# Outer token sums made by adding DMAs on seeded blocks instead of by GpSimd

## The chip, the cores and the metric

The kernel runs on one core of one Trainium2 chip. Its engines work side by side, each through its own list of instructions: PE (TensorE, matrix products), DVE (VectorE), ACT (ScalarE), POOL (GpSimd) and SP (SyncE, which here starts DMAs). All data transfers run on the core's 16 DMA engines. Engines wait for one another through semaphores, and the order on each engine is fixed when the kernel is built. The metric is the device time of the core in microseconds (us). A profiled execution gives the span from the first to the last instruction, and its own time is a little above the span.

## The reference

A layer norm over tokens, a gated linear recurrence, and a routed feed-forward block whose result is scattered by adding. Cut to what matters here:

```python
def _L0_attn_ref(u, a, b, c, d, gate_w, gate_b, d_lr_u, d_lr_v):
    g = jax.nn.sigmoid(jnp.einsum('btd,ed->bte', u, gate_w) + gate_b)
    u_g = u * g
    ...
def _L0_ffn_ref(x, w1, w3, w2, wr):
    xr = x.reshape(-1, D)
    route_probs = jax.nn.softmax(xr @ wr.T, axis=-1)
    routes_k, indices_k = jax.lax.top_k(route_probs, TOP_K)
    gates = routes_k / jnp.sum(routes_k, axis=-1, keepdims=True)
    h = jax.nn.silu(xr @ w1.T)
    h = jax.nn.silu(h @ w3.T)
    h = h @ w2.T
    out = jnp.zeros_like(xr)
    for k in range(TOP_K):
        out = out.at[indices_k[:, k]].add(gates[:, k:k + 1] * h)
    return out.reshape(B, S, D)
x = L0_attn_u                      # (4, 1024, 1024) float32
xn = _layernorm(x, axis=-1)
s = _L0_attn_ref(xn, ...)
g = _silu(_L0_ffn_ref(xn, ...))
x = x + s * g
```

The scatter uses the expert's number as the row, so with 8 experts only the first 8 rows of the 4096 receive anything; all the other rows of the result are rows of the input. The two large products, with `w1` and `w3`, are needed for every token all the same, since every token is added to one of those rows.

## The kernel before

**Work and tiles.** The 4096 tokens are taken in four groups, `sb` = 0 to 3, of 1024. For each group there are a `u` phase (tokens times `w1`, then silu) and an `m` phase (that result times `w3`, silu, then a small scatter product on PE, `acc`). Group 0 also carries the gate product, `g`, between its `u` halves. All values are float32. A *block* is a tile of 128 x 4 x 512 numbers (1 MB); there are 20 of them, `b`. A *quarter* is 128 x 512 (256 KB); there are 24, `q`. A block `o` has four quarters `o[:, 0]` to `o[:, 3]`.

**Fast multiplication in two levels.** Each phase multiplies a 2 x 2 matrix of token blocks (a11, a12, a21, a22; in the code `left[kind, sb, (I, J)]`) by a 2 x 2 matrix of weight blocks with seven products in place of eight. Such a product is a *half* (class `Half`), numbered 1 to 7, and it runs in seven steps, which are the same scheme once more on the quarters of its block; in groups 1 to 3 one of the seven inner products is cut a third time (`eighth`, with `token_thirds` and a weight part `w..._t` that is loaded by `load_thirds`). The halves go in the order 1, 2, 5, 6, 7, 4, 3 in a `u` phase and 1, 5, 6, 2, 7, 4, 3 in an `m` phase.

**Outer token sums.** Four of the halves need a sum of token blocks: half 5 needs s1 = a21 + a22, half 6 needs s2 = s1 - a11, half 3 needs s4 = a12 - s2, and half 7 needs s3 = a11 - a21. The functions `s1`, `s2`, `s4`, `s3` make them, four operations of 128 x 512 each, one for each quarter. In groups 1 to 3 they run on POOL (`s_engine`); s4 is made in place in the block of s2. In group 0 DVE makes them, partly through spare PSUM banks (`with_bank`).

**Inner token sums.** `left_sums` makes four sums of quarters for each half, on POOL in every group, and `token_thirds` three more operations on quarter 1 of the half's block. They read the outer sum, so for halves 3, 5, 6 and 7 they come after it. In the code's terms, `left_sums` is due six places before the half's start and `token_thirds` two before it. In groups 1 to 3 the weight sums come from DRAM: `load_kept` (1 MB, ten places ahead) and `load_kept_sum` (256 KB each).

**What sets the order.** One planner orders everything. `at(place, f, ...)` puts a function on a heap; a function that yields a number goes on so many places later; PE's steps call `run_todo`, and so all instructions of all engines get their order in the program. A half is seven places, and in groups 1 to 3 a place is 1.7 us of PE. A sum is visible to those that read it (`left[kind, sb, "s1"]`, and so on) when the function that makes it has come to its end in this plan; `left_sums` looks again every quarter of a place until it is. Places order the instructions; on the chip an engine runs its list as fast as its semaphores let it. An instruction that waits holds up all that stands behind it on its engine.

**Queues.** Every DMA before the last few is started by SP: loads of tokens for the next group, weights and weight sums, copies of rows of x into the result (`copy_rows`). SP keeps eight in flight; in the full stretches, each start waits for an earlier landing.

Of the kernel before, what the change touches and what calls it, by code (L numbers as in the profile page):

```python
# [13 lines left out]
AF = mybir.ActivationFunctionType  # L14
ALU = mybir.AluOpType
# [7 lines left out]
def kernel(  # L23
# [55 lines left out]
    class Pinned:  # L79
# [16 lines left out]
    pe, dve, act, pool, sync = (  # L96
        Pinned(e) for e in (nc.tensor, nc.vector, nc.scalar, nc.gpsimd, nc.sync)
    )
# [36 lines left out]
    def block(uses=1):  # L135
        return Held(blocks, uses)
# [50 lines left out]
    def at(place, f, *args):  # L187

        seq[0] += 1
        heapq.heappush(todo, (place, seq[0], f, args))  # L190
# [392 lines left out]
    def spare_bank(of=(0, 1)):  # L583


        while not any(n in free_banks for n in of):
            yield 0.25
        taken[0] = next(n for n in free_banks if n in of)
        free_banks.remove(taken[0])
# [3 lines left out]
    def bank_tile(n):  # L593
        if n == 2:
            return ps_sm.tile([P, H], F32, tag="sm", name="spare2")
        return acc if n == 0 else ps_acc.tile([P, H], F32, tag="rows", name="spare")

    def with_bank(out, p, q, order=(0, 1, 2, 3), swap=False, op=ALU.subtract, of=(0, 1)):


        for j in order:
            yield from spare_bank(of)
            n = taken[0]
            ps = bank_tile(n)
            act.copy(ps, q[:, j])
            yield 0.5
            a, b = (ps, p[:, j]) if swap else (p[:, j], ps)
            dve.tensor_tensor(out[:, j], a, b, op)
            free_banks.append(n)
            if of != (0, 1):  # L610
                yield 0.5
# [163 lines left out]
    left = {}  # L775
    left_q = {}

    def s_engine(kind, sb):
        return pool if sb > 0 else dve


    BANKS = {("u", 0): (0, 1), ("m", 0): (0,)}

    def s1(kind, sb, n):
        eng = s_engine(kind, sb)
        a21, a22 = left[kind, sb, (1, 0)], left[kind, sb, (1, 1)]
        o = block(1 + n)
        if (kind, sb) in BANKS:
            yield from with_bank(o, a21, a22, (3, 0, 1, 2), op=ALU.add, of=BANKS[kind, sb])
        else:  # L790
            for q in (3, 0, 1, 2):
                eng.tensor_tensor(o[:, q], a21[:, q], a22[:, q], ALU.add)
                if q == 0:
                    yield 0.5
        a21.drop()
        a22.drop()
        left[kind, sb, "s1"] = o

    def s2(kind, sb, n):
        eng = s_engine(kind, sb)  # L800
        while (kind, sb, "s1") not in left:
            yield 0.25
        p, a11 = left[kind, sb, "s1"], left[kind, sb, (0, 0)]
        o = block(2 * n)
        if (kind, sb) in BANKS:
            yield from with_bank(o, p, a11, (2, 3, 0, 1), of=BANKS[kind, sb])
        else:
            for q in (2, 3, 0, 1):
                eng.tensor_tensor(o[:, q], p[:, q], a11[:, q], ALU.subtract)
                if q == 3:  # L810
                    yield 0.5
        p.drop()
        a11.drop()
        left[kind, sb, "s2"] = o

    def s4(kind, sb, n):

        eng = s_engine(kind, sb)
        while (kind, sb, "s2") not in left:
            yield 0.25  # L820
        o, a12 = left[kind, sb, "s2"], left[kind, sb, (0, 1)]
        if (kind, sb) == ("m", 0):
            yield from with_bank(o, o, a12, (2, 3, 0, 1), True, of=(0, 2))
        else:
            for q in (2, 3, 0, 1):
                eng.tensor_tensor(o[:, q], a12[:, q], o[:, q], ALU.subtract)
                yield 0.5
        a12.drop()
        left[kind, sb, "s4"] = o

    def s3(kind, sb, n):
        eng = s_engine(kind, sb)
        a11, a21 = left[kind, sb, (0, 0)], left[kind, sb, (1, 0)]
        o = block(n)
        if (kind, sb) == ("m", 0):
            yield from with_bank(o, a11, a21, (2, 3, 0, 1), of=(0, 2))
        else:
            for q in (2, 3, 0, 1):
                eng.tensor_tensor(o[:, q], a11[:, q], a21[:, q], ALU.subtract)
                yield 0.5  # L840
        a11.drop()
        a21.drop()
        left[kind, sb, "s3"] = o
# [481 lines left out]
    for kind, sb, i, plain in line:  # L1325
# [3 lines left out]
        n = 2 if sb == 0 and kind == "u" and i not in PLAIN_G else 1  # L1329
# [12 lines left out]
    for sb in range(NS):  # L1342
        n = 2 if sb == 0 else 1
        U = {i: start["u", sb, i] for i in range(1, 8)}
        at(U[5] - (12 if sb > 1 else 7 if sb else 9), s1, "u", sb, n)
        at(U[5] - (9 if sb > 1 else 6), s2, "u", sb, n)
        at(U[7] - 10, s3, "u", sb, n)
        at(U[3] - (13 if sb == 0 else 8.6), s4, "u", sb, n)
        if sb == 0:
            at(U[5] + 2, route, sb)  # L1350
        M = {i: start["m", sb, i] for i in range(1, 8)}
        at(M[5] - 8, s1, "m", sb, 1)
        at(M[5] - 4, s2, "m", sb, 1)
        at(M[7] - 12, s3, "m", sb, 1)
        at(M[3] - 16, s4, "m", sb, 1)
        if sb > 0:
            for r in range(6 if sb < NS - 1 else 4):
                at(U[1] + 14 * r, copy_rows, 6 * (sb - 1) + r)
        if sb + 1 < NS:
            bcs = {}  # L1360
            at(M[1] - (46 if sb == 0 else 40), stats, sb + 1, bcs)
            for k, (I, J) in enumerate(HB):
                at(M[1] + (12 if sb == 0 else 4) + 3 * k, load_xn, sb + 1, I, J, USES[I, J])
            at(M[1] + (17 if sb == 0 else 4), norm, sb + 1, bcs)
            for IJ in HB:
                at(
                    M[1] + 26,
                    lambda sb=sb, IJ=IJ: left.__setitem__(
                        ("u", sb + 1, IJ), xn[(sb + 1,) + IJ]
                    ),  # L1370
                )
# [228 lines left out]
```

## Time and profile before

| | |
|---|---|
| median of 3 runs | 816.02 us (815.76 to 816.16) |
| profiled execution, its time | 816.45 us |
| its span | 814.6 us |
| granted TensorE clock, mean | 0.999 |
| from group 1's scatter to group 2's (286.25 to 460.92) | 174.67 us |
| the same, one group on (460.92 to 637.30) | 176.38 us |
| from there to 802.00 | 164.70 us |
| DMA, whole span | 203.95 MB, mean 250 GB/s |
| POOL, largest four groups, busy | 244.0, 184.5, 152.6, 72.7 us |
| ACT, largest group, mean of one | 696 ns, x152 |

Instructions are grouped by line, engine, operation and tile; since every instruction is recorded in one helper, all have line 89, and the groups are told apart by tile names and shapes: `b` is a block, `q` a quarter, `X`, `Y` and `Z` are the PSUM banks of the products, with the phase behind them (`X_m`). In a row, "out<-in", then the shapes, the count, the busy time and the mean duration in ns, then the engine's idle time ahead of these instructions and what ended it. A row of the timeline begins with the start and the duration in us. In the 40 slices of the page each digit is the busy share of a slice in tenths. A row of DMA issues ends with the median time from issue to landing.

### The profile page before, as it was taken

How to read it: one execution, taken by the hardware profiler on the slowest of the kernel's cores; microseconds unless marked ns; L12 is line 12 of the kernel's file. 1: busy time of each engine (PE TensorE's matmuls, PEld its weight loads, DVE VectorE, ACT ScalarE, POOL GpSimd, SP SyncE). 2: the span in 40 equal slices, each digit the busy share in tenths (PEclk: the TensorE clock that was granted, in tenths of full speed). 3: DMA queues.
4: the chain of work that ended last, by engine and by line, in shares of the span. 5: the costliest groups of instructions: out<-in, count | busy, mean ns of one | idle time of the engine just before them, and what ended most of it. 6: DMA issues, size and time to landing. Idle time of an engine off the chain costs nothing.

```text
span 814.6 us, 12336 instructions
## 1 busy us (share of the span) xinstructions
PE 804.0 (99%) x4337; PEld 698.3 (86%) x4337; DVE 513.9 (63%) x988; ACT 263.6 (32%) x458; POOL 642.2 (79%) x628
## 2 busy tenths in 40 slices
PE   8999999999999999999999999999999999999997
PEld 6888888888888878888888788888888788888884
DVE  5986598766488635744897246735894357656553
ACT  1245126876332228341022165421122021220111
POOL 2799796956999699799999962999498853997820
PEclk9999999999999999999999999999999999999999
DMA  9946609464988939659968967649957567766800
GB/s 336 421 180 233 232 28 359 183 245 138 401 298 284 350 123 341 257 177 389 364 222 325 372 236 263 226 177 388 368 196 291 173 221 244 229 199 203 337 1 2
DMA packets 61980, 203.95 MB, mean 250 GB/s; under 512 B 7152, under 2 KB 10464, under 8 KB 50272
## 3 DMA queue, kind: packets, MB, share of 16 engines
q1 hardware_dynamic: 61600, 202.63, 68.3%
q8 instruction: 35, 0.57, 0.3%
q10 hardware_dynamic: 320, 0.54, 0.2%
q14 instruction: 25, 0.20, 0.1%
HBM read 176.35 MB, written 43.54 MB: 270 GB/s over the span
## 4 chain that ended last, share of the span: by engine, by line
PE 89%; POOL 6%; issue 3%; DMA 2%; DVE 1%; ACT 0%; POOLq 0%; ACTq 0%
PE X_m L89 22%; PE X_u L89 20%; PE Z_m L89 11%; PE Z_u L89 11%; PE X_g L89 6%; PE Y_m L89 5%; PE Y_u L89 5%; POOL q L89 3%; PE Z_g L89 3%; POOL b L89 2%; PE acc L89 2%; PE plT L89 2%; DMA b<-in_x 2%; PE Y_g L89 1%; PE pp L89 0%
## 5 line engine op out<-in xcount | busy, mean ns | idle before, releaser
L89 POOL TENSOR_TENSOR q<-b 128x512 f32<-128x512 f32 (+2 forms) x224 | 244.0, 1106 | 53.3 <-DVE b L89 22.9
L89 ACT ACTIVATE b<-b 128x512 f32<-128x512 f32 (+1 forms) x152 | 105.3, 696 | 299.6 <-DVE b L89 289.3
L89 POOL TENSOR_TENSOR b<-b,b 128x512 f32<-128x512 f32 x120 | 152.6, 1294 | 61.5 <-PE X_u L89 30.0
L89 POOL TENSOR_TENSOR q<-b,q 128x128 f32<-128x128 f32 (+1 forms) x210 | 184.5, 892 | 8.0 <-issue 3.4
L89 PE MATMUL X_m<-q,q 128*128 128x256 f32 x448 | 106.0, 379 | 0.0
L89 PE MATMUL X_u<-q,q 128*128 128x256 f32 x432 | 102.4, 380 | 0.0
L89 PEld LDWEIGHTS X_m<-q,q 128*128 128x128 f32 x448 | 83.4, 190 | 11.3 <-issue 0.8
L89 DVE TENSOR_TENSOR b<-X_u,b 128x512 f32<-128x512 f32 x87 | 60.0, 689 | 51.4 <-PE X_u L89 49.8
L89 PEld LDWEIGHTS X_u<-q,q 128*128 128x128 f32 x432 | 80.2, 190 | 11.1 <-issue 1.2
L89 DVE TENSOR_TENSOR b<-X_m,b 128x512 f32<-128x512 f32 x88 | 60.4, 687 | 40.4 <-PE X_m L89 40.0
L89 POOL TENSOR_TENSOR q<-q,b 128x512 f32<-128x512 f32 x56 | 72.7, 1298 | 12.7 <-PE Z_u L89 12.1
L89 DVE TENSOR_TENSOR b<-b,bc 128x1024 f32<-128x1024 f32 x56 | 67.8, 1211 | 5.2 <-ACT bc L89 5.1
L89 DVE TENSOR_TENSOR b<-b,b 128x512 f32<-128x512 f32 x72 | 69.1, 963 | 3.0
L89 PE MATMUL X_u<-b,b 128*128 128x256 f32 x248 | 58.6, 380 | 0.2
L89 DVE TENSOR_TENSOR b<-Y_m,b 128x128 f32<-128x128 f32 (+1 forms) x112 | 41.4, 385 | 25.2 <-PE Y_m L89 14.8
L89 DVE TENSOR_TENSOR b<-Z_m,b 128x512 f32<-128x512 f32 x48 | 33.0, 688 | 38.1 <-PE Z_m L89 37.7
L89 DVE TENSOR_TENSOR b<-Z_u,b 128x512 f32<-128x512 f32 x47 | 32.4, 689 | 36.7 <-PE Z_u L89 35.8
L89 DVE TENSOR_TENSOR b<-Y_u,b 128x128 f32<-128x128 f32 (+1 forms) x111 | 40.9, 384 | 21.8 <-PE Y_u L89 13.2
L89 PE MATMUL Z_m<-b,q 128*128 128x256 f32 x224 | 53.1, 380 | 0.0
L89 PE MATMUL X_m<-b,b 128*128 128x256 f32 x224 | 53.0, 379 | 0.0
L89 PE MATMUL X_m<-q,b 128*128 128x256 f32 x224 | 53.0, 379 | 0.0
L89 PE MATMUL Z_m<-q,q 128*128 128x256 f32 x224 | 52.9, 379 | 0.0
(194 smaller groups left out, 1317.0 us busy)
## 6 DMA issues: line engine op xcount, KB each, us to landing
q<-w SPq DMA_DIRECT2D x168, 256.0 KB, 4.2
b<-in_w SPq DMA_DIRECT2D x36, 1024.0 KB, 14.9
b<-w_T SPq DMA_DIRECT2D x24, 1024.0 KB, 6.8
b<-in_xT SPq DMA_DIRECT2D x15, 1024.0 KB, 7.3
w<-q SPq DMA_DIRECT2D x56, 256.0 KB, 6.4
b<-in_x SPq DMA_DIRECT2D x12, 1024.0 KB, 10.2
w_T<-b SPq DMA_DIRECT2D x8, 1024.0 KB
q<-w_t SPq DMA_DIRECT2D x28, 256.0 KB, 3.9
```

The source lines that it names most:

```text
L89: r = f(*args, **kwargs)
```

## The change

In groups 1 to 3 the sums s1, s2, s3 and s4 are no longer made by POOL operations. ScalarE copies one of the two inputs into the sum's block, quarter by quarter, with a factor of 1 or -1, and one DMA of 1 MB, started from POOL's queue, adds the other input to what stands there (`accum_op=ALU.add`). That is 23 sums: the `u` phase's s1 of group 1 stays on POOL, with its quarters in another order. s4 takes a block of its own. In group 0 the sums are made as before. Most of the sums start earlier in the plan: in the `u` phases s1 by 5 places (groups 2 and 3), s2 by 4 (6 in group 1), s3 by 4 and s4 by 5.4; in the `m` phases s1 by 3, s2 by 2 and s3 by 3.

```diff
@@ -775,68 +775,87 @@
     left = {}
     left_q = {}
 
-    def s_engine(kind, sb):
-        return pool if sb > 0 else dve
-
 
     BANKS = {("u", 0): (0, 1), ("m", 0): (0,)}
 
+    def seeded(o, seed, sign, other, wait):
+
+        for q in range(4):
+            act.activation(o[:, q], seed[:, q], AF.Copy, scale=sign)
+            yield 0.5
+        while other not in left:
+            yield 0.25
+        yield wait
+        pool.dma_start(o.tile, left[other].tile, accum_op=ALU.add)
+
     def s1(kind, sb, n):
-        eng = s_engine(kind, sb)
-        a21, a22 = left[kind, sb, (1, 0)], left[kind, sb, (1, 1)]
+        a22 = left[kind, sb, (1, 1)]
         o = block(1 + n)
         if (kind, sb) in BANKS:
+            a21 = left[kind, sb, (1, 0)]
             yield from with_bank(o, a21, a22, (3, 0, 1, 2), op=ALU.add, of=BANKS[kind, sb])
+        elif (kind, sb) == ("u", 1):
+            a21 = left[kind, sb, (1, 0)]
+            for q in (3, 2, 0, 1):
+                pool.tensor_tensor(o[:, q], a21[:, q], a22[:, q], ALU.add)
+                yield 0.25
         else:
-            for q in (3, 0, 1, 2):
-                eng.tensor_tensor(o[:, q], a21[:, q], a22[:, q], ALU.add)
-                if q == 0:
-                    yield 0.5
+            yield from seeded(o, a22, 1.0, (kind, sb, (1, 0)), 1)
+            a21 = left[kind, sb, (1, 0)]
         a21.drop()
         a22.drop()
         left[kind, sb, "s1"] = o
 
     def s2(kind, sb, n):
-        eng = s_engine(kind, sb)
-        while (kind, sb, "s1") not in left:
-            yield 0.25
-        p, a11 = left[kind, sb, "s1"], left[kind, sb, (0, 0)]
-        o = block(2 * n)
-        if (kind, sb) in BANKS:
+        if sb > 0:
+            a11 = left[kind, sb, (0, 0)]
+            o = block(2 * n)
+            for q in range(4):
+                act.activation(o[:, q], a11[:, q], AF.Copy, scale=-1.0)
+                yield 0.5
+            while (kind, sb, "s1") not in left:
+                yield 0.25
+            yield 3 if (kind, sb) == ("u", 1) else 4
+            p = left[kind, sb, "s1"]
+            pool.dma_start(o.tile, p.tile, accum_op=ALU.add)
+        else:
+            while (kind, sb, "s1") not in left:
+                yield 0.25
+            p, a11 = left[kind, sb, "s1"], left[kind, sb, (0, 0)]
+            o = block(2 * n)
             yield from with_bank(o, p, a11, (2, 3, 0, 1), of=BANKS[kind, sb])
-        else:
-            for q in (2, 3, 0, 1):
-                eng.tensor_tensor(o[:, q], p[:, q], a11[:, q], ALU.subtract)
-                if q == 3:
-                    yield 0.5
         p.drop()
         a11.drop()
         left[kind, sb, "s2"] = o
 
     def s4(kind, sb, n):
 
-        eng = s_engine(kind, sb)
         while (kind, sb, "s2") not in left:
             yield 0.25
         o, a12 = left[kind, sb, "s2"], left[kind, sb, (0, 1)]
         if (kind, sb) == ("m", 0):
             yield from with_bank(o, o, a12, (2, 3, 0, 1), True, of=(0, 2))
+        elif sb > 0:
+            p, o = o, block()
+            yield from seeded(o, p, -1.0, (kind, sb, (0, 1)), 1)
+            p.drop()
         else:
             for q in (2, 3, 0, 1):
-                eng.tensor_tensor(o[:, q], a12[:, q], o[:, q], ALU.subtract)
+                dve.tensor_tensor(o[:, q], a12[:, q], o[:, q], ALU.subtract)
                 yield 0.5
         a12.drop()
         left[kind, sb, "s4"] = o
 
     def s3(kind, sb, n):
-        eng = s_engine(kind, sb)
         a11, a21 = left[kind, sb, (0, 0)], left[kind, sb, (1, 0)]
         o = block(n)
         if (kind, sb) == ("m", 0):
             yield from with_bank(o, a11, a21, (2, 3, 0, 1), of=(0, 2))
+        elif sb > 0:
+            yield from seeded(o, a21, -1.0, (kind, sb, (0, 0)), 1)
         else:
             for q in (2, 3, 0, 1):
-                eng.tensor_tensor(o[:, q], a11[:, q], a21[:, q], ALU.subtract)
+                dve.tensor_tensor(o[:, q], a11[:, q], a21[:, q], ALU.subtract)
                 yield 0.5
         a11.drop()
         a21.drop()
@@ -1342,16 +1361,16 @@
     for sb in range(NS):
         n = 2 if sb == 0 else 1
         U = {i: start["u", sb, i] for i in range(1, 8)}
-        at(U[5] - (12 if sb > 1 else 7 if sb else 9), s1, "u", sb, n)
-        at(U[5] - (9 if sb > 1 else 6), s2, "u", sb, n)
-        at(U[7] - 10, s3, "u", sb, n)
-        at(U[3] - (13 if sb == 0 else 8.6), s4, "u", sb, n)
+        at(U[5] - (17 if sb > 1 else 7 if sb else 9), s1, "u", sb, n)
+        at(U[5] - (13 if sb > 1 else 12 if sb else 6), s2, "u", sb, n)
+        at(U[7] - (14 if sb else 10), s3, "u", sb, n)
+        at(U[3] - (13 if sb == 0 else 14), s4, "u", sb, n)
         if sb == 0:
             at(U[5] + 2, route, sb)
         M = {i: start["m", sb, i] for i in range(1, 8)}
-        at(M[5] - 8, s1, "m", sb, 1)
-        at(M[5] - 4, s2, "m", sb, 1)
-        at(M[7] - 12, s3, "m", sb, 1)
+        at(M[5] - (11 if sb else 8), s1, "m", sb, 1)
+        at(M[5] - (6 if sb else 4), s2, "m", sb, 1)
+        at(M[7] - (15 if sb else 12), s3, "m", sb, 1)
         at(M[3] - 16, s4, "m", sb, 1)
         if sb > 0:
             for r in range(6 if sb < NS - 1 else 4):
```

## The prediction

> **What bounds the kernel now.** I read first the busy times, then the 40 slices, the groups and the DMA issues, then PE's idle time and the windows around it, and last the chain that leads into the sums concerned. The page, cut to those lines:
>
> ```profile
> PE 804.0 (99%) x4337; PEld 698.3 (86%) x4337; DVE 513.9 (63%) x988; ACT 263.6 (32%) x458; POOL 642.2 (79%) x628
> ...
> DMA  9946609464988939659968967649957567766800
> ...
> L89 POOL TENSOR_TENSOR b<-b,b 128x512 f32<-128x512 f32 x120 | 152.6, 1294 | 61.5 <-PE X_u L89 30.0
> ...
> b<-in_w SPq DMA_DIRECT2D x36, 1024.0 KB, 14.9
> b<-w_T SPq DMA_DIRECT2D x24, 1024.0 KB, 6.8
> b<-in_xT SPq DMA_DIRECT2D x15, 1024.0 KB, 7.3
> ```
>
> PE is busy 804.0 of 814.6 us at full granted clock. POOL, whose work is taken away, is a follower: its 79% cost nothing unless PE waits for it. Between 18 and 800 us the timeline of PE has one idle row:
>
> ```profile
> 561.57 0.46 PE L89 MATMUL Y_m<-q,q 128*128 128x128 f32 x2 [1.37 <-POOL b L89]
> ```
>
> The row names POOL, but POOL's token third for this matmul was done at 550.8. The other operand is a weight third, `w3_6_t`, whose load was issued at 550.2 and landed at 561.4 (11.2 us for 256 KB; the group's median is 4.2 or less in quiet stretches). So the one stall is a late DMA, and less POOL work cannot end it. The windows say why it is late (columns: stretch; length, then busy time and count of PE, PEld, DVE, ACT, POOL; granted clock, DMA share, GB/s):
>
> ```profile
> 360.00:370.00 10.00, 10.00 (x52) 8.79 (x51) 3.00 (x8) 3.34 (x7) 9.85 (x10) 1.00 0.66 224
> 370.00:380.00 10.00, 10.00 (x55) 8.99 (x54) 4.28 (x8) 2.69 (x5) 9.84 (x13) 1.00 0.96 370
> 530.00:540.00 10.00, 10.00 (x54) 8.89 (x53) 4.38 (x10) 3.11 (x5) 9.84 (x11) 1.00 0.01 2
> 540.00:550.00 10.00, 10.00 (x55) 8.99 (x54) 3.15 (x7) 2.38 (x4) 9.92 (x10) 1.00 1.04 386
> 550.00:560.00 10.00, 10.00 (x54) 8.94 (x52) 4.61 (x7) 2.25 (x4) 9.92 (x11) 1.00 0.85 342
> 560.00:570.00 10.00, 8.63 (x43) 7.54 (x43) 5.64 (x10) 1.18 (x2) 9.45 (x11) 1.00 1.04 409
> 720.00:730.00 10.00, 10.00 (x53) 8.99 (x54) 6.02 (x14) 1.91 (x4) 9.84 (x12) 1.00 0.50 172
> ```
>
> From 540 us the 16 DMA engines are full, after ten empty microseconds in which SP waits for the statistics. The same holds around 370 to 402 us one group earlier; group 3 has room (0.50). POOL is full in these stretches too. At the rate of a full stretch, some 409 GB/s, 1 MB takes 2.6 us of all 16 engines.
>
> **The change part by part.** *POOL loses* 23 sums of 4 operations: 92 x 1.294 = 119 us. PE's only gap is not POOL's, so this is worth 0 on the end. It is cover for what follows.
>
> *ScalarE gains* 92 copies of 128x512. The nearest row is an activation of that shape, 0.63 us (below), so 58 us on an engine that is busy 263.6 us and whose largest group waits 289 us for VectorE. The program order of the changed kernel, laid against the old one, is the same for PE, VectorE and SP; ScalarE has only these copies put in. They read blocks ready long before, so they wait for nothing, and a later activation is delayed by at most one or two, 0.63 to 1.3 us, under the 4 us of idle before the activations that matter. I take 0; without cover it would be 1.3 us twice per group.
>
> *DMA gains* 23 transfers of 1 MB that add to their target. None is in this trace. Time on the 16 engines: at least one pass, 2.6 us; with a second read of the target 5.2; with each pass by itself (two reads, one write) 7.8. I take 2.6 to 5.2. Time from issue to landing, D: below, the fastest plain 1 MB load (4.9 us, issued 540.0); above, the slowest in a full stretch (13.1 us, issued 550.8) plus a second pass, 15.7. In a quiet stretch I take 5.0 + 2.6 = 7.6, in a full one 10 to 13, as most rows of such stretches are (7.5 to 13.1 for loads behind others). The Trainium skill (DMA: Bandwidth & Descriptors, section "Issuing engines are not separate DMA queues") speaks against the change here: a DMA started from POOL runs on the same 16 engines as SP's and interleaves with them. The full windows above are where that would bite; no transfer of POOL is in this trace to show it. The same skill (Collectives: The Full Stack, section on the bandwidth ceiling) has an add read two sources on one ring, with a measured ratio of 1.93 to a plain copy; by it the quiet D would be an estimated 1.93 x 5.0 = 9.7 us and all terms below would lie in their upper halves; no row here has an add.
>
> *The new waits.* In the old kernel POOL adds a quarter as soon as its input is there. Now the whole sum starts with its last quarter and ends with a landing. That matters where the input is late: the `m` half 5, whose first sum needs the block (1,0) just out of ScalarE's silu:
>
> ```profile
> 357.77 0.63 ACT L89 ACTIVATE b<-b 128x512 f32<-128x512 f32 x1 [4.17 <-DVE b L89]
> ...
> 532.44 0.63 ACT L89 ACTIVATE b<-b 128x512 f32<-128x512 f32 x1 [4.17 <-DVE b L89]
> ...
> 708.82 0.63 ACT L89 ACTIVATE b<-b 128x512 f32<-128x512 f32 x1 [3.89 <-DVE b L89]
> ```
>
> These end at 358.4, 533.1 and 709.5; only then can the DMA of s1 go. What is queued behind it on POOL: the inner sums of half 5, which read the landed block, so POOL stands for D. Then come 11 operations (8.6 us by their old durations) in group 1, 7 (6.8 us) in groups 2 and 3, then the DMA of s2, another D, and behind that, since the next operation reads s2, two operations (2.5 us) that make half 5's third inner sum. PE wants that sum at 385.6, at 560.5 (561.9 less the stall) and at 736.8, and s2 itself at 383.4, 558.1 and 734.6. Group 1: 385.6 - 358.4 - 8.6 - 2.5 = 16.1 us are left for two landings, less 0 to 1.5 for issuing (two issues at up to 0.7, about twice an SP issue). Groups 2 and 3: 18.1 and 18.0, so 16.5 to 18.1. Hence the stall is 2D less these, and the point from which it bites is a mean D of 7.3 to 8.1 us in group 1, 8.2 to 9.1 in the others.
>
> - Group 1: s1 goes into a stretch of share 0.66, 7.6 to 10; s2 into one of 0.96, 10 to 13. Sum 17.6 to 23 less 14.5 to 16.1: 1.5 to 8.5 us. I take 3, the low side, as loads issued just ahead of it landed in 5.
> - Group 2: s1 meets the empty stretch, 7.6; s2, issued at about 548, the full one, 10 to 13. Sum 17.6 to 20.6 less 16.5 to 18.1: -0.5 to 4.1. In the same place the load that already stalls PE by 1.4 is behind s2's transfer and comes 2.6 to 5.2 later. Both delay the same matmuls, so the larger counts: 2.6 to 5.2; I take 4.
> - Group 3: 15.2 to 18 less 16.5 to 18: 0 to 1.5. I take 0.5.
>
> The other sums (all of the `u` phases, s3, s4) are first used 12 to 30 us after they could be issued, beyond the 10 to 13 of a full stretch: 0; with 15.7 still 0 to 4 in the tightest one. s4 takes a block of its own where it worked in place: SP's loads get waits on ScalarE's copies and on landings, all past by the old times but one load at 461.3 that waits to 464.0 and has 29 us to spare: 0. The moved starts change POOL's order only; no DMA of SP moves, so no queue is passed by another.
>
> Sum: 3 + 4 + 0.5 = 7.5 us. On the profiled execution 816.45 would be 824.0 (its span 814.6, with 1.85 around it); the median of the runs is 816.02, 0.43 less, so 823.5; an engine that is 99% busy makes nothing of it up, but the three terms can share half a microsecond with the 1.37 us already lost at 560, and I give 823.
>
> **The rivals.** *The cover holds, no change.* If the add runs along with the copy, D is near the plain 5 to 7 us, below the 7.3 from which anything is late, and only the load at 561 moves. Then 814.6 (the 1.37 us gone because the order of traffic changes) to 817.6 (one more pass before it); 816.0. For it: 5.0 us for the load of 364.8. Against: the full stretches, where 1 MB loads that were not first in line took 7.5 to 13. This is the case on the other side: not slower, one mechanism, with its point at D = 7.3.
>
> *Faster beyond what can be told.* 0.2% (1.6 us) is about what a measurement of this kernel can tell from no change. The single stall is 1.37 us, so this needs it gone and something in the first 18 or last 13 us besides, which the change doesn't touch. 814.
>
> *DMA becomes the bound.* DMA shares over the three periods are 0.77 of 174.7 us, 0.74 of 176.4 and 0.56 of 164.7: 134.5, 130.5 and 92.2 us. With 7, 8 and 8 sums at 5.2 us they become 171, 172 and 134: just under the periods. At 7.8 us they are 189, 193 and 155, and groups 1 and 2 are 14.5 and 16.5 too long: 816 + 31 = 847. For it: three passes are what the data needs if nothing overlaps. Between, with D = 13 in groups 1 and 2 and 10 in 3: 26.2 - 15.3, 26.2 - 17.3 and 20 - 17.3, or 10.9 + 8.9 + 2.7 = 22.5, 838.5.
>
> *It doesn't do what it says*: POOL may stand waiting for as long as it saves. POOL has 119 us less work and up to 23 x 10 of landings to wait for; but beyond the `m` half 5 the plan puts other work between, so this is in the terms already.
>
> **How the numbers follow.** Forecast (817.6 to 830, point 823): 0.48. Hidden: 0.27. DMA-bound or long D (830 to 850): 0.19. Faster: 0.06. So slower 0.67, same 0.27, faster 0.06. The range is 814.5 to 842: it takes in the hidden case and the middle of the long one, and leaves out the far end of that and of the faster one. The forecast's own range is 817.6 to 830.
>
> **What would show it.** In the changed profile: PE idle at about 385 and 560, ended by POOL or a DMA in `m` half 5 to 6; POOL idle for D after the silus at 358 and some 174 us later; adds landing in 7 to 8 us quiet and 10 to 13 in full stretches; DMA share up by 0.1 to 0.2 in each period; ScalarE up by about 58 us, POOL down by 119. I am wrong if adds land in under 7 us in the full stretches, if a load of weights sets the stalls instead, or if PE waits in a `u` phase.

## The result and the profile after

The changed kernel takes 840.6 us (839.12 to 842.87) beside 816.07 us before (the table's 816.02 with one more run): a ratio of 1.0304, 95% interval 1.0276 to 1.0331. It is 24.5 us slower, where 7 us was forecast. The profiled execution took 842.87 us, the slowest of four, with a span of 841.1 us, 26.5 us more than before. From its page:

```profile
PE 813.1 (97%) x4337; PEld 704.0 (84%) x4337; DVE 511.7 (61%) x988; ACT 310.0 (37%) x550; POOL 543.0 (65%) x559
...
DMA  9936629465987899799988999699989698875920
...
q0 software_dynamic: 3312, 24.12, 14.1%
...
b<-in_w SPq DMA_DIRECT2D x36, 1024.0 KB, 18.2
...
b<-b POOLq DMA_DIRECT2D x23, 1024.0 KB, 11.3
```

POOL lost 99 us of work where 119 was forecast, because starting the 23 DMAs is work of its own, 0.85 to 1.01 us each. ScalarE gained 46 us where 58 was forecast. The new queue's packets filled 14.1% of 16 engines' span: 0.141 x 841.1 / 23 = 5.2 us of all 16 engines for each 1 MB add. In the windows over the three periods (286.18 to 468.36, 468.36 to 653.88, 653.88 to 824.67 us) the DMA share is 0.90, 0.95 and 0.73, where it was 0.77, 0.74 and 0.56.

PE, which had one idle row between 18 and 800 us, now has eight. Its timeline, each row that begins behind idle time:

```profile
386.37 0.89 PE L89 MATMUL X_m<-b,b 128*128 128x256 f32 x3 [2.91 <-issue]
...
391.26 0.57 PE L89 MATMUL Y_m<-q,q 128*128 128x128 f32 x2 [2.71 <-POOL q L89]
...
568.34 0.45 PE L89 MATMUL X_m<-b,b 128*128 128x256 f32 x1 [2.57 <-issue]
...
573.93 0.35 PE L89 MATMUL Y_m<-q,q 128*128 128x128 f32 x1 [2.10 <-DMA q<-w_t]
...
588.73 0.46 PE L89 MATMUL Y_m<-q,q 128*128 128x128 f32 x2 [2.63 <-DMA q<-w_t]
...
753.91 0.38 PE L89 MATMUL Y_m<-q,q 128*128 128x128 f32 x1 [0.57 <-POOL q L89]
...
764.09 0.35 PE L89 MATMUL Y_m<-b,q 128*128 128x128 f32 x1 [0.83 <-DVE b L89]
...
796.60 0.76 PE L89 MATMUL Y_m<-q,q 128*128 128x128 f32 x2 [4.82 <-DMA q<-w_t]
```

The brackets add up to 19.1 us, 17.8 more than before. The rows at 386 and 568 say "issue", but these matmuls are the first of `m` half 6, which reads s2, and by the trace's semaphores s2's add landed at 386.28 and 568.25, 0.1 us ahead of them. The rows with `w_t` are weight thirds: `w3_6_t`, `w3_2_t`, `w3_4_t`.

That leaves some 9 us, and they are in PE's busy time: 813.1 for 804.0, for the same 4337 instructions. The windows around the second stall show them (columns as in the prediction):

```profile
384.70:388.10 3.40, 1.73 (x8) 1.58 (x9) 0.68 (x2) 0.00 (x0) 1.69 (x2) 1.00 1.03 366
388.10:391.50 3.40, 0.69 (x6) 0.47 (x5) 0.69 (x1) 0.00 (x0) 3.40 (x5) 1.00 1.01 422
391.50:395.00 3.50, 3.50 (x10) 2.80 (x10) 0.49 (x2) 0.00 (x0) 3.34 (x7) 0.51 1.02 414
395.00:398.40 3.40, 3.40 (x17) 3.01 (x16) 3.19 (x4) 0.00 (x0) 3.40 (x4) 1.00 0.98 359
```

From 391.5 to 395 PE is busy without a gap and gets through 10 instructions in place of 20: its granted clock is 0.51. The trace's clock records have four such stretches in groups 1 to 3, three of 3.41 us and one of 6.83; each begins behind a stall or inside one. PE works for 14.2 of these 17.1 us and stands for the others, so half speed costs it 7.1 us. Of the other 2 us of busy time, 1.0 lies in the first 30 us, where PE idles that much less. Idle and busy time make 17.8 + 9.1 = 26.9 us; the rest, -0.4, is idle time in the first 18 us and behind the last matmul.

Followed matmul by matmul against the old trace, PE falls behind by 7.6 us in group 1 (at `m` half 6), by 9.1 in group 2 (4.8 at half 6, 4.3 at half 2) and by 9.2 in group 3 (4.8 of idle and 2.3 of clock at half 4).

### The profile page after: what moved, and what is told of

Same layout as the page of the kernel before. It is cut to its first block, busy times and chain, and to the rows that moved or that the text cites. A ratio compares the mean times of both kernels' runs of the same rounds, so it can differ in the third digit from the quotient of the medians.

```text
span 841.1 us, 12428 instructions
## 1 busy us (share of the span) xinstructions
PE 813.1 (97%) x4337; PEld 704.0 (84%) x4337; DVE 511.7 (61%) x988; ACT 310.0 (37%) x550; POOL 543.0 (65%) x559
## 3 DMA queue, kind: packets, MB, share of 16 engines
q0 software_dynamic: 3312, 24.12, 14.1%
## 4 chain that ended last, share of the span: by engine, by line
PE 42%; DMA 8%; issue 2%; POOL 1%; DVE 1%; SPq 0%; ACT 0%; POOLq 0%
PE X_m L89 12%; PE X_u L89 11%; PE Z_u L89 6%; DMA q<-w_t 6%; PE Z_m L89 5%; PE Y_u L89 2%; PE Y_m L89 2%; DMA b<-b 2%; PE acc L89 1%; POOL q L89 1%; DMA q<-w 1%; PE plT L89 1%; DVE y L89 1%; PE pp L89 0%; DVE b L89 0%
## 5 line engine op out<-in xcount | busy, mean ns | idle before, releaser
L89 POOL TENSOR_TENSOR q<-b 128x512 f32<-128x512 f32 (+2 forms) x224 | 249.3, 1139 | 189.6 <-DMA b<-b 100.3
L89 ACT ACTIVATE b<-b 128x512 f32<-128x512 f32 (+1 forms) x244 | 155.9, 667 | 284.0 <-DVE b L89 258.3
L89 PE MATMUL X_m<-q,q 128*128 128x256 f32 x448 | 110.6, 392 | 0.0
L89 PEld LDWEIGHTS X_m<-q,q 128*128 128x128 f32 x448 | 86.2, 197 | 12.4 <-issue 0.8
L89 POOL TENSOR_TENSOR q<-q,b 128x512 f32<-128x512 f32 x56 | 75.5, 1348 | 0.2
L89 DVE TENSOR_TENSOR b<-b,b 128x512 f32<-128x512 f32 x72 | 64.9, 905 | 2.7
L89 POOL DMA_DIRECT2D b<-b x23 | 20.3, 882 | 56.7 <-ACT b L89 28.6
L89 DVE TENSOR_TENSOR b<-Y_u,b 128x128 f32<-128x128 f32 (+1 forms) x111 | 40.9, 384 | 23.2 <-PE Y_u L89 13.1
```

Source lines behind the costliest of these rows:

```text
L89: r = f(*args, **kwargs)
```

## The experiments

### Which sums, and through what

**m12_pool**: six of the 23 sums go back.

```diff
+        elif kind == "m":
+            a21 = left[kind, sb, (1, 0)]
+            for q in (3, 0, 1, 2):
+                pool.tensor_tensor(o[:, q], a21[:, q], a22[:, q], ALU.add)
...
+        if sb > 0 and kind == "m":
...
+            for q in (2, 3, 0, 1):
+                pool.tensor_tensor(o[:, q], p[:, q], a11[:, q], ALU.subtract)
...
-        at(M[5] - (11 if sb else 8), s1, "m", sb, 1)
-        at(M[5] - (6 if sb else 4), s2, "m", sb, 1)
+        at(M[5] - 8, s1, "m", sb, 1)
+        at(M[5] - 4, s2, "m", sb, 1)
```

> The changed kernel, but s1 and s2 of the three m phases (6 of the 23 sums) are made by POOL again, at their old places. Theory 'chain' (the stalls at m half 5 and 6 come from two landings one after the other behind a late silu): the steps of PE's delay there, 7.7 us in group 1 with its slow clock, 4 in group 2, 1.7 in group 3, go, and 840.6 becomes 825 to 828; the weight-third stalls of 2.1 to 2.6 us in group 2 and of 4.8 us in group 3 are still there at least in part. Rival 'traffic' (PE waits in proportion to what the added transfers take of the 16 DMA engines): 6 of 23 transfers are worth 6 of 24.6 us, 834. Rival 'fixed order' (the other 17 sums do the harm): within 2 us of 840.6.

Measured: 819.37 us, ratio 1.0045 (1.0031 to 1.0060). That is more than any of the theories gave: 21.2 of the 24.5 us go with six transfers, and the 4.8 us stall of group 3, which lies nearer to s3's and s4's adds, goes with them. Two stalls are left, in PE's timeline:

```profile
561.38 0.46 PE L89 MATMUL Y_m<-q,q 128*128 128x128 f32 x2 [1.47 <-POOL q L89]
...
576.17 0.46 PE L89 MATMUL Y_m<-q,q 128*128 128x128 f32 x2 [2.63 <-DMA q<-w_t]
```

The first is the one of before, the second is `w3_2_t`, which had 2.4 us to spare in the old kernel. So the other 17 adds cost 3.6 us.

**m12_dma_only**: the complement, the kernel before with only these six sums by seed and DMA (the added code is that of the change, for `kind == "m" and sb > 0`).

> The complement: the kernel before, with only s1 and s2 of the m phases of groups 1 to 3 made by seeds and adding DMAs at the changed kernel's places, everything else on POOL. 'Chain': the steps at m half 5 and 6 appear as in the changed kernel, 816 + 13 = 828 to 831, with no stall at the group 3 weight third (w3_4_t). 'Traffic': 816 + 6.4 = 822.5. Should the two parts not add up to 24.6 us, what is missing is shared DMA time.

Measured: 834.03 us, ratio 1.0227 (1.0210 to 1.0244): 18.3 us, above both. Stalls of 2.99 and 1.07 us at half 6 of group 1, 2.27 at half 6 and 2.05 at its weight third in group 2, 1.98 at half 2 of group 1, and four windows of slow clock. The two complements make 3.6 + 18.3 = 21.9 of 24.5. Neither has the stall of group 3, 4.8 us and two slow windows, so that one takes both parts.

**seeds_pool_adds**: ScalarE's copies and the new places stay, POOL adds in place of the DMA.

```diff
-        pool.dma_start(o.tile, left[other].tile, accum_op=ALU.add)
+        for q in (2, 3, 0, 1):
+            pool.tensor_tensor(o[:, q], o[:, q], left[other][:, q], ALU.add)
```

> The changed kernel's seeds on ScalarE and its places, but POOL adds into the seeded block (four operations in place) where the DMA was. If ScalarE's 92 copies and the new order cost nothing, as the prediction has it: 815 to 818, PE's idle time as before. Rival 'ScalarE' (the copies hold up silus or the scatter): a rise of 3 us or more with PE waiting for sums behind late silus. POOL does its old work, so its adds behind the late silu could bring up to 2 us by themselves.

Measured: 815.90 us, ratio 1.0006 (0.9997 to 1.0016), ScalarE busy 310.0 us as in the changed kernel. The 92 copies and the new order cost nothing that can be seen.

**copy_not_add**: the same transfers from the same queue as plain copies. The addition is left out, so the sums are not those of the reference.

```diff
-        pool.dma_start(o.tile, left[other].tile, accum_op=ALU.add)
+        pool.dma_start(o.tile, left[other].tile)
```

> The changed kernel with each of the 23 adding DMAs turned into a plain copy of the same 1 MB from the same queue: the addition is left out, so the sums and the result are not the reference's. Same instructions, same waits. Theory 'two passes' (an add costs a second read, 5.2 us of 16 engines against 2.6): the software queue's share falls from 14.1% to about 7%, landings come 2.5 to 4 us earlier, the stall of group 1 shrinks by some 5 to 8 us and the weight thirds' stalls vanish or halve: 820 to 827. Rival 'latency' (a POOL-issued transfer is late whatever it does): shares as in a plain load, landings within 1 us of the adding ones, 837 to 841.

Measured: 823.41 us, ratio 1.0091 (1.0074 to 1.0108). Its queue line:

```profile
q0 software_dynamic: 3312, 24.12, 7.5%
```

The same packets and bytes as above, and 7.5% in place of 14.1%. By the packets in the trace, a plain copy takes 2.5 us of all 16 engines where they are full and an add 5.03; from issue to the last packet a copy takes 4.4 to 12.0 us and an add 7.2 to 13.1. The instructions and waits are those of the changed kernel, so 17 of the 24.5 us hang on the addition, which doubles what a transfer takes of the engines.

### Waits or traffic

**side_by_side**: all 23 transfers stay, but s2 no longer waits for s1.

```diff
+            o2 = block(2 * n)
+                pool.tensor_tensor(o2[:, q], a22[:, q], a11[:, q], ALU.subtract)
...
+            pool.dma_start(o.tile, a21.tile, accum_op=ALU.add)
+            pool.dma_start(o2.tile, a21.tile, accum_op=ALU.add)
```

> The changed kernel with all its 23 adding DMAs, but in the m phases s2 no longer waits for s1: POOL makes a22 - a11 ahead of time in s2's block (12 operations more in all, 15 us of POOL), and when a21 is there two DMAs go one right behind the other, each adding a21, one to s1's block and one to s2's. Same transfers, same bytes, but their two landings overlap and half 5's third inner sum is no longer behind s2's. Theory 'chain in series': s1 lands by 370 us in group 1, the steps of 7.7 us (group 1), 4 (group 2) and 1 to 2 (group 3) go, 840.6 becomes 827 to 830. Theory 'traffic': the DMA load is the same, so within 3 us of 840.6.

Measured: 840.79 us, ratio 1.0295 (1.0265 to 1.0325). The expectation of "chain in series" fell. The stall in front of half 6 of group 1 is gone, but there is one of 2.7 us at half 5 (s1's DMA started 3.2 us later, as POOL had the subtractions ahead of it), one of 3.0 us behind half 6 (half 2's 1 MB weight load, which landed 0.1 us ahead of the matmul, though its row names ScalarE), and 3.0 and 9.6 us at `w3_5_t` and `w3_6_t` in group 2.

**after_thirds5** moves one kind of load:

```diff
-            at(S - 3, *((weight_thirds if sb == 1 else load_thirds), kind, sb, i))
+            at(S - (5 if sb > 1 and kind == "m" else 3), *((weight_thirds if sb == 1 else load_thirds), kind, sb, i))
```

> The changed kernel, with one thing moved: in the m phases of groups 2 and 3 the load of the weight third (256 KB) is due 5 places ahead of its half in place of 3, which puts it ahead of about three other loads in SP's queue. Theory 'late in the queue': the stalls at w3_6_t, w3_2_t (group 2) and w3_4_t (group 3) with the slow clock behind the last two, some 12 us, shrink to what is left of the chain: 828 to 832. Theory 'the 16 engines are short of time': what is moved ahead makes something else late by as much, 837 to 841. The stalls of group 1 stay in both.

Measured: 830.18 us, ratio 1.0185 (1.0168 to 1.0202), 10.4 us below the changed kernel and inside "late in the queue". The stalls at `w3_2_t` and `w3_4_t` are gone, and with them three of the five slow windows (of 3.41 us each). At the matmul that reads `w3_6_t` 0.6 us is left, for which POOL's sum and no longer the load is the last to come. The stalls at half 6 stay: 2.91 and 1.44 us in group 1, 2.05 in group 2.

**side_dve** is side_by_side with DVE in POOL's place for the subtraction, and the loads of after_thirds5.

```diff
-                pool.tensor_tensor(o2[:, q], a22[:, q], a11[:, q], ALU.subtract)
+                dve.tensor_tensor(o2[:, q], a22[:, q], a11[:, q], ALU.subtract)
```

> side_by_side once more with its two disturbances taken out: a22 - a11 is made by DVE (so that POOL is free to start s1's DMA when the silu ends; in side_by_side it started 3.2 us later in group 1), and the weight thirds are loaded 5 places ahead. To be compared with after_thirds5, 830.2, which has the same transfers. 'Chain in series' says its idle at m half 5 to 6 (2.91 + 1.44 in group 1, 2.05 + 0.61 in group 2) and two slow-clock windows of 1.7 go, 10 us: 819 to 823. 'Traffic' says that two adds at once (10 us of 16 engines) make loads late by as much: 828 or more. A third reading, DVE now drains PSUM late: PE waits for PSUM with DVE as the releaser.

Measured: 831.91 us, ratio 1.0209 (1.0191 to 1.0226): what "traffic" said. The row that replaces the chain's in group 1:

```profile
399.92 1.19 PE L89 MATMUL X_m<-b,b 128*128 128x256 f32 x2 [3.93 <-DMA b<-in_w]
```

No idle is left at halves 5 and 6 there, and 12 us later PE stands for a 1 MB weight load, which landed 6.3 us before its use in the old kernel. In group 2 the stalls are at weight thirds again, 3.2 and 1.8 us. The third reading has a small part: PE waits 0.6 and 1.1 us with DVE as the releaser, near the ends of the silus of groups 2 and 3.

**one_landing** is after_thirds5 with s1 of the `m` phases on POOL, as in m12_pool, and s2 left to the DMA.

> after_thirds5 with s1 of the m phases on POOL again and only s2 by seed and DMA: one landing in the chain, 20 transfers. 'Chain in series': in group 1 the s1 sums are done some 5 us after the silu in place of 9.2, so the chain is 4 to 5 us shorter; of 2.91 + 1.44 in group 1 and 2.05 + 0.61 in group 2 nothing or under 1 us is left, and no slow window: 820 to 824 against 830.2. 'Traffic': 3 of 23 transfers less, 828 to 830.

Measured: 830.22 us, ratio 1.0188 (1.0171 to 1.0205), no gain; a miss for the chain as I had drawn it. The add of s2 was issued 6 us earlier in group 1 than in the changed kernel (369.9 in place of 376.1), but its last packet came 14.6 us after that, at 384.5, where it had been 385.9; PE still lost 1.48 and 2.71 us there. Its first packet moved 7.0 us after the issue; in a quiet stretch it is 1.5. In this full stretch the backlog of the DMA engines set the landing, hardly the issue.

**traffic_only**: the kernel before, with POOL making every sum, and six adds into spare blocks that nobody reads.

```diff
+        if kind == "m" and sb > 0:
+            spare = block()
+            pool.dma_start(spare.tile, a21.tile, accum_op=ALU.add)
+            spare.drop()
```

> The kernel before with POOL making every sum as it did, and beside that six adding DMAs of 1 MB into spare blocks, one right behind s1 and one behind s2 in the three m phases: the transfers of m12_dma_only (834.0) with nobody reading what they make. It does more than the kernel needs; its result is the reference's. 'The wait' (PE loses time because sums arrive by a landing): 816 to 818. 'Traffic' (1 MB adds take 5 us of 16 engines each and loads come late, whoever waits): 828 to 834, with PE stopped by loads. Both in part: about 821 to 825, stalls at the weight thirds of group 2.

Measured: 831.11 us, ratio 1.0174 (1.0157 to 1.0191): most of m12_dma_only's loss with no sum waiting for a landing. PE's timeline in groups 1 and 2:

```profile
392.94 2.73 PE L89 MATMUL X_m<-q,q 128*128 128x256 f32 x8 [1.92 <-DMA q<-w]
...
574.34 0.77 PE L89 MATMUL Y_m<-q,q 128*128 128x128 f32 x2 [8.43 <-DMA q<-w_t]
```

Both wait for weights (a third stall, 1.35 us at half 5 of group 1, is put down to POOL, which now stands for a21 to start the first add). SP issued `w3_6_t` at 561.7 in place of 550.2, behind landings that the adds had pushed back. In group 3, where the windows had room, the same two adds cost no idle at all.

**rows_early**: the changed kernel, with the two copies of rows that fall into the `m` phases of groups 1 and 2 moved to the `u` phases.

```diff
-                at(U[1] + 14 * r, copy_rows, 6 * (sb - 1) + r)
+                at(U[1] + (14 * r if r < 4 else 14 * r - 49), copy_rows, 6 * (sb - 1) + r)
```

> The changed kernel with the two copies of rows of x (1 MB each, read and written) that fall into the m phases of groups 1 and 2 due 49 places earlier, in the u phases. Nothing of the sums' chain is touched. 'Traffic': some 2.6 us of 16 engines less per copy in the full stretches, so s2 and the weight thirds land earlier there and 840.6 becomes 832 to 837. 'The wait' alone: 839 to 842. If the u phases can't hold the copies, 843 or more.

Measured: 840.07 us, ratio 1.0293 (1.0276 to 1.0310), which is what the other theory said. The stall at half 6 of group 2 fell from 2.57 to 1.0 us, but its weight third's rose from 2.10 to 2.9, and half 5 and 6 of group 1 lost 4.7 us as against 5.6. Relieving the engines of these copies did not pay; why a copy counts for so little beside an add I have not tried.

**traffic_only_thirds5** and **m12_dma_only_thirds5** take the weight thirds' lateness out of both halves, with the move of after_thirds5.

> traffic_only (831.1; six adds nobody reads) with the weight thirds of the m phases loaded 5 places ahead in place of 3. If traffic hurts by the place of one load in SP's queue, the 8.4 us stall at w3_6_t and its three slow-clock windows (5 us) go: 818 to 821, what is left being group 1 (1.4 + 1.9 and one slow window). If the DMA engines are short of time in the whole stretch, another load takes its place: 826 or more.

> m12_dma_only (834.0; the same six transfers as real sums) with the same move. If the wait for two landings is a loss of its own, the stalls at half 6 stay (2.99 + 1.07 in group 1, 2.27 in group 2, with their slow windows): 826 to 831, 6 us or more above traffic_only_thirds5. If the wait is only another face of the traffic, the two agree within 3 us.

Measured: 822.67 us, ratio 1.0077 (1.0060 to 1.0094), and 831.10 us, ratio 1.0177 (1.0160 to 1.0194). They do not agree: 8.4 us lie between the same six transfers with and without somebody waiting for their sums, and the transfers alone cost 8.5 us beside the old kernel with the same move (814.22, before_thirds5 below). So neither expectation for traffic_only_thirds5 was met; it came between them. The rows that differ, of m12_dma_only_thirds5:

```profile
386.35 0.77 PE L89 MATMUL X_m<-b,b 128*128 128x256 f32 x1 [3.23 <-issue]
...
568.88 0.45 PE L89 MATMUL X_m<-b,b 128*128 128x256 f32 x1 [2.29 <-issue]
```

and of traffic_only_thirds5, at about the same places (its profiled execution was the slowest of four, 826.09 us, so its stalls are larger than usual):

```profile
392.95 0.45 PE L89 MATMUL X_m<-q,q 128*128 128x256 f32 x1 [1.87 <-DMA q<-w]
...
567.96 0.55 PE L89 MATMUL Y_m<-q,q 128*128 128x128 f32 x1 [3.24 <-DMA q<-w_t]
```

The first pair waits for s2 in half 6 (with five windows of slow clock behind it), the second for weights. So the wait is a loss of its own. It and the traffic's own loss lie in the same stretches and overlap: side_dve and one_landing took parts of the wait away and gained nothing.

### The prediction's own claim on the kernel before

**before_thirds5** is the kernel before, with the edit of after_thirds5 and nothing else.

> The same move in the kernel before. The prediction held that PE's one stall there, 1.37 us at 560, is w3_6_t's landing and not POOL. If so it goes: 0.8 to 1.4 us less, 814.4 to 815.2, with no idle of PE between 18 and 800 us. If POOL is its cause, as the row names it: 815.7 and the stall stays.

Measured: 814.22 us (813.53 to 815.04), ratio 0.9979 (0.9970 to 0.9988). The window that had 8.63 us of PE is full, with POOL as busy as ever:

```profile
560.00:570.00 10.00, 10.00 (x53) 8.94 (x52) 6.22 (x11) 1.18 (x2) 9.68 (x11) 1.00 1.03 402
```

This version beats both kernels. **m12_pool_thirds5** gives 17 sums to the DMA as well.

> m12_pool (17 sums by DMA, s1 and s2 of the m phases on POOL) with the weight thirds' loads earlier as well. There only two stalls were left, 1.5 us at w3_6_t and 2.6 us at w3_2_t in group 2. Theory: both are late loads, so 819.4 becomes 815 to 816.5, no better than the earlier load alone in the kernel before, since nothing waits for POOL. Rival: the added traffic makes other loads late, 818 or more.

Measured: 816.85 us, ratio 1.0012 (1.0003 to 1.0020), 2.6 us above before_thirds5 with POOL busy for 569 us in place of 643, and a stall of 2.07 us at a weight third still there. Between its theory and its rival, nearer to the first.

## Why the prediction was wrong

The profiled execution is 26.5 us longer. The waits that the sum's three terms stood for (3, 4 and 0.5 us) came to 5.9, 4.8 and 0.6. The rest are stalls at two weight thirds and the slow clock, which the sum put at nothing or did not have.

**The bound and the one stall: right.** before_thirds5 shows that the stall at 560 was the load `w3_6_t`, although its row named POOL. POOL's lost work and ScalarE's copies were worth nothing, as said (seeds_pool_adds).

**The price of an add: right for the landing, at the upper end for the engines.** Taken: 7.6 us to landing in quiet stretches, 10 to 13 in full ones, 2.6 to 5.2 us of 16 engines. By the packets of the changed kernel: 7.2 to 8.7, 9.8 to 13.1, and 5.03 to 6.07 (in the experiments up to 15.5 us to landing). The Trainium skill's rule that I had set against the change (DMA: Bandwidth & Descriptors, "Issuing engines are not separate DMA queues") holds here: in traffic_only, where POOL's adds do nothing else, SP's `w3_6_t` landed at 574.2 in place of 561.4, while PE had fallen behind by only 5.7 us.

**Group 1, 3 us taken of 1.5 to 8.5: the mechanism right, the term mis-sized.** POOL's timeline in the changed kernel:

```profile
358.63 0.90 POOL L89 DMA_DIRECT2D b<-b  x1 [0.73 <-ACT b L89]
367.84 2.49 POOL L89 TENSOR_TENSOR q<-b 128x512 f32<-128x512 f32 x2 [8.31 <-DMA b<-b]
...
376.14 0.87 POOL L89 DMA_DIRECT2D b<-b  x1
386.41 2.49 POOL L89 TENSOR_TENSOR q<-b 128x512 f32<-128x512 f32 x2 [9.40 <-issue]
388.87 1.25 POOL L89 TENSOR_TENSOR q<-q,b 128x512 f32<-128x512 f32 x1
390.09 1.12 POOL L89 TENSOR_TENSOR q<-b 128x128 f32<-128x128 f32 x2
```

The two steps from a DMA row to the next operation are 9.2 and 10.3 us, in the range taken. I had two operations behind the second landing (half 5's third inner sum). What PE waits for at 391.26 is half 6's token third, which ends at 391.21, so 4.8 us of POOL stand there in place of 2.5. With that the budget is 385.4 - 358.4 - 8.6 - 4.8 = 13.6 us, and 19.5 us of landings give the 5.9 us by which PE falls behind there, before the clock adds 1.7.

**Group 2, 4 us: right at half 6; the zero for "the other sums" failed at half 2.** At half 6 PE falls behind by 4.8 us, inside the 2.6 to 5.2 taken. It waits 2.57 us for s2 and then 2.10 us for `w3_6_t`, which lands 15.7 us after its start in place of 11.2, with s2's add among the transfers ahead of it. That load was started at 558.15, before PE stood for s2, so the later of the two landings sets the delay, as taken. What failed is the term "The other sums: 0". It asked when s3 and s4 are read, and not which loads share the engines with their adds. `w3_2_t` had 2.4 us to spare (landed at 571.12, read at 573.57). In the changed kernel it starts at 573.82, and s3's add, started at 577.34, runs beside it: it takes 14.8 us to land in place of 9.7, and PE stands for 2.63 us with 1.7 us of slow clock behind. m12_pool, which has s3's add but not s2's, has the same 2.63 us.

**Group 3, 0.5 us: the same zero failed, in two ways.** The chain gave 0.57 us, as taken, and 0.83 more went to DVE, busy with the recurrence just then. The other 4.82 us, and 2.3 us of slow clock, are `w3_4_t`, which had 10.5 us to spare before (landed at 762.61, read at 773.08). POOL and SP in the changed kernel:

```profile
770.58 2.51 POOL L89 TENSOR_TENSOR q<-b 128x512 f32<-128x512 f32 x2 [7.13 <-DMA b<-b]
774.24 0.31 POOL L89 MEMSET b<- 128x256 f32 x1
...
758.30 0.38 SPq L89 DMA_DIRECT2D b<-w_T x1
774.58 1.35 SPq L89 DMA_DIRECT2D b<-in_x  x4
...
780.51 0.42 SPq L89 DMA_DIRECT2D q<-w_t  x1
```

SP's loads at 774.58 go into a block that POOL clears first (the MEMSET). POOL comes to that late, since it has stood 7.28, 7.38 and 7.13 us for s1, s2 and s3 to land. So SP stands for 16.3 us from one start to the next, where it was 5.0 (and 6.6 in traffic_only, where POOL waits for no landing), and from its next start to PE's need of `w3_4_t` there are 17.2 us in place of 27.3. Then s4's add starts at 780.52, in the same instant as this load, and the load takes 16.0 us to land. Neither alone is enough. With s1 and s2 on POOL (m12_pool) SP stands 6.0 us, and the load has 7.8 us to spare. Without s4's add (m12_dma_only) SP stands 14.6 us, but the load lands in 9.4 and has 1.7 us to spare. The prediction's "POOL may stand waiting ... this is in the terms already" missed SP's wait for POOL. after_thirds5, which only starts these loads earlier, takes the stall away.

**Not in the sum at all: the slow clock.** Of the 7.1 us that it costs PE, 1.4 lie ahead of the wait for `w3_6_t`, which would have ended no sooner without them. The other 5.7 us are nearly a quarter of the loss. A stall of 3 us, the size forecast for group 1, comes to 4.7 with a slow window behind it.

One sign of being wrong that the prediction had named did come: loads of weights set three of the stalls. Nearest in number was the sum with two landings of 13 us in groups 1 and 2 and of 10 in group 3, 838.5. That is luck: measured were 9.2 and 10.3 us in group 1 and 7.4 and 13.0 in group 2, and it has no stall at a weight third. The rival in which DMA becomes the bound (847) does not hold as a sum either: an add took 5.03 to 6.07 us of 16 engines in place of 7.8, and over a period the engines stay below full (0.90, 0.95, 0.73). But it was right in kind for the 30 to 50 us of the `m` phases of groups 1 and 2 in which they were full before the change. There an add of 5 us pushes back the loads beside and behind it, and `w3_6_t` and `w3_2_t` had less than that to spare. What stays open is how the backlog is shared out: rows_early took two transfers from those stretches and won nothing.

## What to carry to other kernels

An engine that is 79% busy and on which PE never waits gives nothing when its work is taken away. Look first at what takes the work over, and here that was full in just the stretches where the sums are wanted. Look also at who else waits for that engine: once POOL stood for landings, SP stood for POOL. Price a new transfer against the slack of every load beside and behind it in the stretch, one by one, not against the mean share; and add a penalty for the clock to each stall of two microseconds or more. Where PE's only stall is a load, moving that load ahead in its queue (1.65 us here, for one number) beats relieving the engine that the row names.

## What the runs showed of the hardware

**A stall of 2 to 3 us can cost half as much again or more.** The slow stretches of the clock in groups 1 to 3 are 3.41 us long or multiples of it. Laid on that grid, a window with 1.92 us or more of PE idle was followed by one at half clock, in the changed kernel and in all the experiments, while a full-clock window with 1.89 us or less was not: 2.71 us in one window brought it on, and 2.91 us shared as 1.26 and 1.65 between two did not. A slow window in which PE works throughout costs 1.7 us. The Trainium skill (TensorE: Matmul & The Clock Gate, section "HAM oscillation — how this bites in real kernels") gives as the rule that idle gaps should not exceed about 3.4 us. Gaps of 2 to 3 us were enough here, by where they fell.

**An adding DMA takes twice the engine time of a copy,** 5.03 against 2.48 us of 16 engines for 1 MB between blocks, where both ran in full stretches, and 0.87 against 0.57 us of POOL to start.
